# A graph layer on one core: five of 49 destination blocks gathered row by row, 44 packed

## The chip, the cores and the metric

The kernel runs on one core of a Trainium2 chip. The metric is the device time of one launch in microseconds (us). The other seven cores do nothing.

## The reference

One message-passing layer with two edge types, a residual and a layer norm, over N = 6250 nodes of 128 features and E = 100,000 edges sorted by destination:

```
Xs  = x[src]
msg = where(edge_type == 0, Xs @ W_data.T + b_data, Xs @ W_control.T + b_control)
agg = segment_sum(msg, dst)                      # per destination node
out = relu(agg + x @ W_self.T + b_self)
y   = layernorm(x + out)                         # per node, eps 1e-5
```

## The kernel before

**Blocks and tables.** The nodes are cut into NB = 49 blocks of P = 128. In a lead-in, TensorE computes both message vectors of every node, `x @ W + b`, and the kernel splits each fp32 result into three bf16 parts. They lie side by side as 384 columns (D3) in SBUF, tile `m3[:, s, :]`, with NT = 98 source tiles: 49 blocks for each of the two edge types. A copy goes to DRAM as `table`, one row of 768 bytes per (type, node). The parts of x themselves are stored to DRAM as `x3_t`. `load_x`, `split_x`, `multiply`, `take`, `leave`, `store_x` and `store` are the lead-in; its pools close at the step `built`.

**Windows.** Since edges are sorted by destination, the edges of a destination block lie in a window of WIN = 2304 edges (KT = 18 columns of 128), whose first edge the kernel finds itself (`starts`). SP loads a window per block (`win`).

**Packing.** Blocks are worked in groups, `GROUPS = (4,) + (5,) * 9`. For each group the kernel builds a packing: one-hot tiles of the source tile of each edge (`hot_st`, line L548), a running rank of each edge among those with the same source tile (matmuls with `tri` and `rest` into `acc`, read by VectorE into `slot`, L565), and from these, with the matmuls of L603, the packed lists: for each source tile 32 slots, each with a source row and a destination row. ScalarE copies them (L616, L636), and SP stores `packed` to DRAM. Edges of rank 32 or more are listed as spills; GpSimd fetches their messages from `table` with an indirect DMA of 32 rows (`msg_s`, L693).

**A packed block.** SP broadcasts the block's packed list to all partitions (`rows`, 784 KB, L718). VectorE turns it into one-hot matrices (L725, `select`) and makes the destination's one-hots in two chunks (`hot_d`, L739, `to_hots`). Then come NS = 25 tiles. In each, four matmuls gather four source tiles' messages out of `m3` into a PSUM tile `g_ps` (L752, `gather`; GB = 5 buffers), ScalarE evicts it as bf16 `gs` (L760, `evict`), and four matmuls, one for each 32 columns of the array (`by_columns`, L220), add it into the block's sum `agg` (`add_up`). The block's own product `x @ W_self` is added from `x_p`, which SP loads from `x3_t` (L781, `load_own`, `own_of`); a last product adds spills and bias. VectorE adds the three parts (L142), adds x and relu (L138) into the group's tile `h_p` and takes its statistics. After a group, `normalise` applies the norm on ScalarE (L179), and SP stores `h_p` (L186).

**The order.** Each engine runs its instructions in order. Nothing in the program text fixes that order: the functions are generators of steps, and the class `Order` simulates five engines ("T", "V", "A", "G", "S" for TensorE, VectorE, ScalarE, GpSimd and SP) with costs written in each step. It always issues the step that can start earliest and, among those that can start within `CLOSE` of it on that engine, the one with the earliest due time (function `due`, from BUILT = 85 and BLOCK per block). A step names the steps that it needs; a step with two engines in its costs goes to the one that is free first. So the whole instruction stream of the chip follows from these costs and due times, and a transfer or an engine that is slower than planned holds up whatever stands behind it. The semaphores between engines follow from the buffers.

**Buffers.** The pool `late`, opened at `built`, has one buffer of each tile unless `bufs` is given: `h_p` has one, `x_p` and `xs_p` four (XS), `hot_d` four, `gs` eight. `rows` has four (RB). Each of the eight PSUM banks is in use: three for `small`, `acc` and `agg`, five for `g_ps`.

Of the kernel before, what the change touches and what calls it, by code (L numbers as in the profile page):

```python
# [19 lines left out]
P = 128  # L20
# [12 lines left out]

GROUPS = (4,) + (5,) * 9
Q = max(GROUPS)
NPG = len(GROUPS)
STARTS = [sum(GROUPS[:i]) for i in range(NPG)]
R = 32
NS = (NT + 3) // 4
NC = 4 * NS  # L40
RB = 4
M = 8
SLOT = 128.0
PARTS = (4, 8, 8, 8, 8, 8, 5)
KC = 6
DC = 13
# [3 lines left out]
class Order:  # L50
# [9 lines left out]
    AFTER = 0.25  # L60
    CLOSE = 0.2

# [38 lines left out]
def kernel(  # L101
# [24 lines left out]


    nc = tc.nc
    dram = ctx.enter_context(tc.tile_pool(name="dram", bufs=1, space=DRAM))
    const = ctx.enter_context(tc.tile_pool(name="const", bufs=1))  # L130
    table = dram.tile([NT * P, D3], BF16, name="table")
    x3_t = dram.tile([NB, D, 3 * P], BF16, name="x3_t")
    packed = dram.tile([NB, NT * R], BF16, name="packed")
    total = const.tile([1, 1], I32, name="total")
# [69 lines left out]
def sums_over_windows(ctx, tc, x, xt, edges, w, bias, table, x3_t, packed, total,  # L204
# [3 lines left out]
    const = ctx.enter_context(tc.tile_pool(name="consts", bufs=1))  # L208
    work = ctx.enter_context(tc.tile_pool(name="work", bufs=2))
    row_pool = ctx.enter_context(tc.tile_pool(name="row_pool", bufs=RB))  # L210
    ps_a = ctx.enter_context(tc.tile_pool(name="ps_a", bufs=1, space=PSUM))
# [30 lines left out]
    counted = {}  # L242
    for n in sorted({DC, *GROUPS}):
        counted[n] = const.tile([P, P, n], BF16, name=f"count{n}")
        G.iota(counted[n], pattern=[[1, P], [0, n]], base=0, channel_multiplier=0,
               allow_small_or_imprecise_dtypes=True)
# [34 lines left out]
    def three_parts(parts, whole, left):  # L281
# [17 lines left out]
    spill_tiles = [(const.tile([P, Q * P], BF16, name=f"hot_s{i}"),  # L299
                    const.tile([P, D3], BF16, name=f"msg_s{i}")) for i in range(2)]  # L300
    slot_values = [const.tile([P, (Q + 1) // 2, NC], BF16, name=f"vs{i}") for i in range(2)]
    slot_b = {n: const.tile([P, R, n], BF16, name=f"slot{n}") for n in sorted({*GROUPS})}

    def constants():
# [23 lines left out]

        for hot, msg in spill_tiles:
            V.memset(hot, 0.0)  # L330
            V.memset(hot[R : R + 1, :], 1.0)
            V.memset(msg, 0.0)
            V.tensor_copy(msg[R : R + 1, :].rearrange("p (i c) -> p i c", i=3),
                          parts[0:1, :, 2 * D :])

    win = {}
    first = const.tile([1, NB], I32, name="first")
    counts = const.tile([P, NPG], F32, name="counts")
    m3 = const.tile([P, NT, D3], BF16, name="m3")
    m3v = m3.rearrange("p (t b) c -> p t b c", t=2)  # L340

    def starts():
# [12 lines left out]
        V.tensor_scalar_min(first, first_ps[:1, :NB], float(E - WIN))  # L355
        for b in range(NB):
            grp = [g for g in range(NPG) if STARTS[g] <= b][-1]
            yield step(("win", b), {"S": 0.84}, "first", *([("fields", grp - 2)] if grp > 1 else []),
                       lag=2.0)
            if b == STARTS[grp]:  # L360
                win[grp] = work.tile([P, Q, KT, 3], I32, name="win")
            at = nc.values_load(
                first[0:1, b : b + 1], engines=(SP,), min_val=0, max_val=E - WIN,
                skip_runtime_bounds_check_because="it counts edges and is held to E - WIN",
            )
            nc.sync.dma_start(
                win[grp][:, b - STARTS[grp], :, :],
                edges[ds(at, WIN), :].rearrange("(p k) c -> p k c", p=P),
            )
# [8 lines left out]
    LEAD, BUILT = 12.0, 85  # L378
    BLOCK = 13.5
    AHEAD = 12.0  # L380

    def due(kind, *i):
        if kind in ("p", "g") and i[0] in ("root", "rooted", "scale", "apply", "out"):
            n = i[1] + 1
            return BUILT + 10 + BLOCK * sum(GROUPS[:n])
        if kind in ("counted", "turned", "first"):
# [13 lines left out]
        if kind in ("win", "xs", "agg", "o", "whole", "sum"):  # L400
            b = i[0]
            begun = BUILT + BLOCK * b
            if kind == "win":
                return begun - 2 * BLOCK * GROUPS[1] - 20
            return begun + {"whole": BLOCK + 0.5, "sum": BLOCK + 3}.get(kind, 0.3 * BLOCK)
        if kind in ("rows", "sel", "d", "g", "e", "s"):
            of = {"rows": 1, "sel": 1, "d": 2}.get(kind, NS)
            lead = {"rows": -9, "sel": -3, "d": -1, "g": 0, "e": 1, "s": 2}[kind]
            return BUILT + BLOCK * (i[0] + (i[1] / of if len(i) > 1 else 0)) + lead
        n = GROUPS[i[0]]  # L410
        end = BUILT + BLOCK * STARTS[i[0]] - AHEAD
# [14 lines left out]
    def load_x():  # L426
        for g, n in enumerate(PARTS):
            yield step(("xt", g), {"A": 0.45}, *([("x3", g - 3)] if g > 2 else []), lag=4.0)
            xts[g] = build.tile([D, max(PARTS), P], F32, name="xt", bufs=3)[:, :n]
            A.dma_start(xts[g].rearrange("p b c -> p (b c)"),  # L430
                        xt[:, at_part[g] * P : (at_part[g] + n) * P])
# [21 lines left out]
    def multiply():  # L453
        for i, (g, b, n) in enumerate(two_blocks):
            free = [("yl", two_blocks[i - YB][1])] if i >= YB else ["biased"]
            yield step(("y", b), {"T": 1.08 * n}, ("x3", g), *free)
            ys[b] = y = ps_y.tile([P, 2, 2 * D], F32, name="y")
            for j in range(n):
                for i in range(3):
                    for k in range(3):  # L460
                        T.matmul(y[:, j, :], x3s[g][:, b + j - at_part[g], i, :],  # L461
                                 w3[:, k, : 2 * D], start=i == j == k == 0, stop=False,
                                 skip_group_check=True)
                T.matmul(y[:, j, :], ones_b, bias3, start=False, stop=True, skip_group_check=True)  # L464

# [242 lines left out]
    d_hots, g_tiles, gs_tiles, aggs, xss, x3b, hs_, mvs = {}, {}, {}, {}, {}, {}, {}, {}  # L708
    XS = 4
    DB, EB, GB = 4, 8, 5  # L710

# [9 lines left out]
    def select():  # L721

        for b in range(NB):
            yield step(("sel", b), {"V": 1.2}, ("rows", b))
            V.tensor_scalar(rows[b], rows[b], pid1, None, op0=ALU.is_equal)  # L725

    def to_hots():
        tiles = [(b, c) for b in range(NB) for c in range(-(-NS // DC))]
        for i, (b, c) in enumerate(tiles):
# [12 lines left out]

    tiles = [(b, g) for b in range(NB) for g in range(NS)]

# [10 lines left out]
    def evict():  # L755
        for i, (b, g) in enumerate(tiles):
            free = [("s", *tiles[i - EB])] if i >= EB else []
            e = yield step(("e", b, g), {"A": 0.37}, ("g", b, g), *free)
            gs_tiles[b, g] = gs = late.tile([P, D3], BF16, name="gs", bufs=EB)
# [15 lines left out]

    def load_own(name, blocks):
        for i, b in enumerate(blocks):
            free = [("sum", blocks[i - XS])] if i >= XS else []
            yield step(("xs", b), {"S": 0.9}, ("rows", b), "built", *free, lag=4.0)
            x3b[b] = late.tile([D, 3, P], BF16, name=f"x3_{name}", bufs=XS)  # L780
            nc.sync.dma_start(x3b[b].rearrange("p i c -> p (i c)"), x3_t[b])  # L781
            xss[b] = load_rows(b, late, f"xs_{name}", XS)

    def own_of(blocks, begun):

        for i, b in enumerate(blocks):
            yield step(("agg", b), {"S": 0.0}, *([("whole", blocks[i - 1])] if i else []))
            yield step(("o", b), {"T": 0.5}, ("xs", b), begun(b))
            for i in range(3):
                by_columns(aggs[b].rearrange("p (i c) -> p i c", i=3), x3b[b][:, i, :],  # L790
                           w3[:, :, 2 * D :], start=False, stop=False, skip_group_check=True)

    def finish_blocks():
        for b, (grp, q) in enumerate(blocks):
# [3 lines left out]
            if q == 0:  # L798
                hs_[grp] = late.tile([P, Q, D], F32, name="h_p")
                mvs[grp] = work.tile([P, Q, 2], F32, name="mv_p")  # L800
# [16 lines left out]


    late = ps_g = None

    def close_build():
        nonlocal late, ps_g
        yield step("built", {"S": 0.0}, "stores", ("yl", NB - 1), *[("x3_t", g) for g in range(len(PARTS))])
        early.close()
# [9 lines left out]
        take(1, "ym", "y1"), leave(1, "y2", "ym"), take(2, "yl", "y2"), constants(), store_x(), store(), close_build(),  # L834
        load_own("p", list(range(NB))), own_of(list(range(NB)), lambda b: ("s", b, 0)),
    ], due)


    total_ps = ps_a.tile([P, 512], F32, name="small")
    T.matmul(total_ps[:1, :NPG], ones[:, 0:1], counts, start=True, stop=True)  # L840
    total_f = work.tile([1, 1], F32, name="total_f")
    V.tensor_reduce(total_f, total_ps[:1, :NPG], axis=AX.X, op=ALU.add)
    V.tensor_copy(total, total_f)
# [121 lines left out]
```

## Time and profile before

| | before |
|---|---|
| device time, median of three runs | 721.98 us (721.96 to 722.43) |
| the profiled execution | 718.77 us, its span 717.1 us |
| TensorE busy, weight loads | 667.4 us (93%), 574.3 us (80%) |
| VectorE, ScalarE, GpSimd busy | 527.5 us (74%), 572.6 us (80%), 23.3 us (3%) |
| granted TensorE clock | 0.99 |
| DMA | 73.05 MB, 102 GB/s on average |

Device time contains the span from the first to the last instruction and a little around it. Busy time is the time in which an engine executes; matmuls are pipelined, so a TensorE that is always busy can still be waiting for its partner engines between tiles. In the group lines, "out<-in" names the tiles, "x1225" counts instructions, then come the busy time and the mean duration of one in ns, and after the second bar the idle time just before them and who ended it. In the timelines, the first two numbers are start and duration in us, and the bracket at the end is idle time before the instruction and the one that ended it.

### The profile page before, as it was taken

Reading aid. Unit: us, or ns where it says so; the run is one execution under the profiler, and the core shown is the slowest. Engines: PE = TensorE matmul, PEld = TensorE weight load, DVE = VectorE, ACT = ScalarE, POOL = GpSimd, SP = SyncE. Lnnn points to the kernel's source line nnn. Section 1 sums busy time; section 2 is a strip of 40 time slices with the busy share of each in tenths; the row PEclk is TensorE's granted clock in tenths of the full one; section 3 lists DMA queues with packets and bytes.
Section 4 is the critical chain, followed back from the end, with each engine's and each line's share of the span. In section 5 each row is a group of like instructions: output and inputs, shape, how many; then the busy total and the mean of one; then the engine's idle time right before and its main releaser. Section 6 shows DMA issues by size and latency. Waiting matters only on the chain.

```text
span 717.1 us, 33878 instructions
## 1 busy us (share of the span) xinstructions
PE 667.4 (93%) x14698; PEld 574.3 (80%) x14698; DVE 527.5 (74%) x1101; ACT 572.6 (80%) x1407; POOL 23.3 (3%) x21
## 2 busy tenths in 40 slices
PE   3799979999999999999989989999999999999993
PEld 2667747898898888889878888998988897887882
DVE  8565568788869958886985888699689778657321
ACT  3666546889789887888978888898889888798994
POOL 4000000000000000000000000000000000001000
PEclk9999989999999999999999999999999999999997
DMA  5566564053006105301710530160062026006200
GB/s 162 163 209 217 165 212 155 9 170 124 11 15 243 52 3 193 108 8 45 222 42 4 202 97 9 42 235 24 4 222 76 4 92 201 7 4 222 75 4 23
DMA packets 57564, 73.05 MB, mean 102 GB/s; under 512 B 12292, under 2 KB 50191, under 8 KB 57359
## 3 DMA queue, kind: packets, MB, share of 16 engines
q1 hardware_dynamic: 55806, 66.70, 28.6%
q10 hardware_dynamic: 1154, 3.41, 1.5%
q8 instruction: 116, 1.90, 1.1%
q0 software_dynamic: 448, 0.72, 0.3%
q14 instruction: 40, 0.33, 0.2%
HBM read 52.85 MB, written 17.96 MB: 99 GB/s over the span
## 4 chain that ended last, share of the span: by engine, by line
PE 57%; DVE 24%; DMA 10%; ACT 3%; issue 3%; SPq 1%; DVEq 0%; ACTq 0%
PE agg L220 21%; PE g_ps L752 17%; PE acc L220 7%; PE small L603 5%; DVE slot L565 4%; DMA x_p<-x_t 4%; DMA out<-h_p 4%; PE y L461 4%; DVE hot_d L739 4%; DVE hot_st L548 3%; DVE two L586 3%; ACT h_p L179 2%; DVE rows L725 1%; DVE hr L581 1%; PE y L480 1%
## 5 line engine op out<-in xcount | busy, mean ns | idle before, releaser
L760 ACT CAST gs<-g_ps 128x384 bf16<-128x384 f32 x1225 | 489.5, 514 | 67.9 <-PE g_ps L752 61.5
L220 PE MATMUL agg<-gs,hot_d 128*32 128x384 bf16 x4900 | 407.1, 332 | 2.8 <-ACT gs L760 1.9
L752 PE MATMUL g_ps<-m,rows 128*32 128x384 bf16 x4900 | 399.9, 328 | 3.1 <-DVE rows L725 2.8
L220 PEld LDWEIGHTS <-hot_d 128*32 128x32 bf16 x4900 | 232.5, 137 | 28.4 <-issue 5.9
L752 PEld LDWEIGHTS <-rows 128*32 128x32 bf16 x4900 | 217.0, 137 | 22.6 <-issue 5.6
L565 DVE TENSOR_REDUCE slot<-acc 128x5 bf16<-128x490 f32 (+1 forms) x180 | 117.5, 653 | 78.7 <-PE acc L220 76.1
L739 DVE TENSOR_TENSOR hot_d<-count,to 128x1664 bf16<-128x1664 bf16 x98 | 104.6, 1068 | 11.4 <-PE agg L220 9.1
L220 PE MATMUL acc<-hot_st,rest 128*32 128x490 bf16 (+1 forms) x680 | 72.8, 375 | 13.7 <-DVE slot L565 13.2
L220 PE MATMUL acc<-hot_st,tri 128*32 128x490 bf16 (+1 forms) x720 | 77.7, 370 | 1.3 <-DVE hot_st L548 1.3
L548 DVE TENSOR_TENSOR hot_st<-count,st_b 128x2940 bf16<-128x2940 bf16 (+1 forms) x30 | 58.8, 1964 | 16.0 <-PE small L603 8.1
L473 ACT CAST m<-y 128x512 bf16<-128x512 f32 (+1 forms) x75 | 40.5, 580 | 31.7 <-PE y L464 23.8
L603 PE MATMUL small<-hot_st,two 128*32 128x98 bf16 x1764 | 64.9, 291 | 0.0
L461 PE MATMUL y<-w,x 128*128 128x256 bf16 x441 | 57.8, 279 | 6.1 <-DVE w L283 3.2
L603 PEld LDWEIGHTS <-two 128*32 128x32 bf16 x1764 | 60.4, 118 | 0.9 <-issue 0.2
L220 PEld LDWEIGHTS <-rest 128*32 128x32 bf16 x680 | 30.5, 96 | 34.1 <-issue 30.3
L461 PEld LDWEIGHTS <-x 128*128 128x128 bf16 x441 | 43.7, 100 | 13.3 <-issue 3.2
L725 DVE TENSOR_SCALAR rows<-rows,pid 128x3136 bf16<-128x3136 bf16 x49 | 50.2, 1024 | 4.0 <-DMA rows<-packed 3.9
L142 DVE TENSOR_REDUCE whole<-agg 128x128 f32<-128x384 f32 x49 | 27.1, 553 | 34.6 <-PE agg L220 33.3
L220 PE MATMUL agg<-w,x_p 128*32 128x384 bf16 x588 | 36.4, 327 | 4.0 <-DMA x_p<-x_t 3.6
L693 POOL DMA_INDIRECT msg_s<-table,row_i x10 | 14.7, 1475 | 630.1 <-PE g_ps L752 484.6
L220 PEld LDWEIGHTS <-x_p 128*32 128x32 bf16 x588 | 20.7, 97 | 9.2 <-DMA x_p<-x_t 5.4
L220 PEld LDWEIGHTS <-tri 128*32 128x32 bf16 x720 | 24.5, 97 | 2.8 <-issue 2.1
(123 smaller groups left out, 369.5 us busy)
## 6 DMA issues: line engine op xcount, KB each, us to landing
rows<-packed SPq DMA_DIRECT2D x49, 784.0 KB, 6.7
table<-m SPq DMA_DIRECT2D x10, 768.0 KB, 4.2
x_p<-x_t SPq DMA_DIRECT2D x49, 96.0 KB, 7.1
x_t<-x SPq DMA_DIRECT2D x5, 768.0 KB, 7.7
xs_p<-in_x SPq DMA_DIRECT2D x49, 64.0 KB, 6.5
xt<-in_xt ACTq DMA_DIRECT2D x5, 512.0 KB, 4.4
out<-h_p SPq DMA_DIRECT2D x8, 320.0 KB, 3.9
win<-in_edges SPq DMA_DIRECT2D x49, 27.0 KB, 1.9
```

Of the source, the lines that this page charges most:

```text
L142: nc.vector.tensor_reduce(whole, agg.rearrange("p (i c) -> p c i", i=3), axis=AX.X, op=ALU.add)
L220: T.matmul(out[c : c + 32], lhsT[:, c : c + 32], rhs, **flags)
L461: T.matmul(y[:, j, :], x3s[g][:, b + j - at_part[g], i, :], w3[:, k, : 2 * D], start=i == j == k == 0, stop=False, skip_group_check=True)
L473: A.copy(part_of(b, n, i), ys[b][:, :n, :].rearrange("p b (t c) -> p t b c", t=2))
L548: V.tensor_tensor(hot, counted[n][:, None, 1 : NT + 1, :].to_broadcast([P, KC, NT, n]), fields[grp][2][:, c * KC : c * KC + KC, None, :].t ...
L565: V.tensor_reduce(slots[grp][:, k, :], by_q, axis=AX.X, op=ALU.max)
L586: V.tensor_tensor(two[:, :, i], hr, f[:, ks, None, :].to_broadcast(wide), op=ALU.mult)
L603: T.matmul(vt[c0 : c0 + R, q // 2, :], two[:, k, i, :, q], hot[:, k, :, q], start=c == k == 0 and q < 2, stop=c * KC + k == KT - 1, skip_g ...
L725: V.tensor_scalar(rows[b], rows[b], pid1, None, op0=ALU.is_equal)
L739: V.tensor_tensor(hot, counted[DC][:, :, :n], places[grp][:, q, None, c * DC : c * DC + n].to_broadcast([P, P, n]), op=ALU.is_equal)
L752: T.matmul(g_ps[t * R : (t + 1) * R, :D3], rows[b][:, :, s], m3[:, s, :], start=True, stop=True)
L760: (A.copy if e == "A" else V.tensor_copy)(gs, g_tiles.pop((b, g))[:, :D3])
```

## The change

Five destination blocks (44 to 48) are no longer packed. For each of them GpSimd fetches the messages of its 18 edge columns, 128 rows of `table` at a time, with an indirect DMA into `msg` (three buffers); VectorE makes one-hots of the destinations, six columns at a time (`hot_g`); and four matmuls per column add them into a sum of its own, `agg_g`. The own product and the bias (from `hot_b`, `msg_b`) are added as before. Their windows are loaded after those of the first two groups. In the plan a gather takes 5.8 us of GpSimd (PACE), so that the 90 gathers are spread over 522 us of it. The five blocks are normalised and stored together.

The packed groups become `(4,) + (5,) * 8`. `agg_g` takes a PSUM bank, and `g_ps` has four. `rows` has three buffers, `xt` two. `x_p` and `xs_p` are in a pool of their own, opened at the start, and wait for the part of `x3_t` that they read and for an older tile, not for `built` and `rows`. `h_p` has two buffers. The bias matmuls of a pair of blocks come after the products of both, and the first pairs need the step `bias`, no longer `biased`. In the last group an eviction may go to VectorE. CLOSE goes from 0.2 to 0.1 and BLOCK from 13.5 to 13.2. The diff, cut to what matters:

```diff
-GROUPS = (4,) + (5,) * 9
+GROUPS = (4,) + (5,) * 8
+NPB = sum(GROUPS)
+NG = NB - NPB
-RB = 4
+XS = 4
+RB = 3
+CH = 6
-    CLOSE = 0.2
+    CLOSE = 0.1
...
+    own_pool = ctx.enter_context(tc.tile_pool(name="own_pool", bufs=1))
...
-        for b in range(NB):
-            grp = [g for g in range(NPG) if STARTS[g] <= b][-1]
-            yield step(("win", b), {"S": 0.84}, "first", *([("fields", grp - 2)] if grp > 1 else []),
-                       lag=2.0)
+        for b in [*range(STARTS[2]), *range(NPB, NB), *range(STARTS[2], NPB)]:
+            grp = [g for g in range(NPG) if STARTS[g] <= b][-1] if b < NPB else NPG
+            free = [("fields", grp - 2)] if 1 < grp < NPG else []
+            yield step(("win", b), {"S": 0.84}, "first", *free, lag=2.0)
...
-    BLOCK = 13.5
+    BLOCK = 13.2
+    PACE = 5.8
...
+        if kind in ("gh", "gm", "msg"):
+            k = i[1] * CH if kind == "gh" else i[1]
+            return BUILT + PACE * (i[0] * KT + k) + {"msg": 0, "gh": 2, "gm": 5}[kind]
...
-            yield step(("xt", g), {"A": 0.45}, *([("x3", g - 3)] if g > 2 else []), lag=4.0)
-            xts[g] = build.tile([D, max(PARTS), P], F32, name="xt", bufs=3)[:, :n]
+            yield step(("xt", g), {"A": 0.45}, *([("x3", g - 2)] if g > 1 else []), lag=4.0)
+            xts[g] = build.tile([D, max(PARTS), P], F32, name="xt")[:, :n]
...
-            free = [("yl", two_blocks[i - YB][1])] if i >= YB else ["biased"]
+            free = [("yl", two_blocks[i - YB][1])] if i >= YB else ["bias"]
...
+            for j in range(n):
                 T.matmul(y[:, j, :], ones_b, bias3, start=False, stop=True, skip_group_check=True)
...
-    DB, EB, GB = 4, 8, 5
+    DB, EB, GB = 4, 8, 4
...
-            e = yield step(("e", b, g), {"A": 0.37}, ("g", b, g), *free)
+            costs = {"A": 0.37, "V": 0.53} if b >= STARTS[-1] else {"A": 0.37}
+            e = yield step(("e", b, g), costs, ("g", b, g), *free)
...
-            free = [("sum", blocks[i - XS])] if i >= XS else []
-            yield step(("xs", b), {"S": 0.9}, ("rows", b), "built", *free, lag=4.0)
-            x3b[b] = late.tile([D, 3, P], BF16, name=f"x3_{name}", bufs=XS)
+            part = [g for g in range(len(PARTS)) if at_part[g] <= b][-1]
+            free = [("sum", blocks[i - bufs])] if i >= bufs else []
+            yield step(("xs", b), {"S": 0.9}, ("x3_t", part), *free, lag=4.0)
+            x3b[b] = own_pool.tile([D, 3, P], BF16, name=f"x3_{name}", bufs=bufs)
...
-                hs_[grp] = late.tile([P, Q, D], F32, name="h_p")
+                hs_[grp] = late.tile([P, Q, D], F32, name="h_p", bufs=2)
...
+    def gather_rows():
+        for i, (j, k) in enumerate(gathered):
+            free = [("gm", *gathered[i - MB])] if i >= MB else [*stored, "built", "idx"]
+            yield step(("msg", j, k), {"G": PACE}, *free, lag=3.0 - PACE)
+            msgs[j, k] = late.tile([P, D3], BF16, name="msg", bufs=MB)
+            G.indirect_dma_start(
+                out=msgs[j, k], out_offset=None, in_=table[:, :],
+                in_offset=bass.IndirectOffsetOnAxis(ap=idx[:, j, k : k + 1], axis=0),
+            )
+
+    def gathered_hots():
...
+            yield step(("gh", j, c), {"V": 0.55}, ("msg", j, c * CH), *free)
+            g_hots[j, c] = hot = late.tile([P, P, CH], BF16, name="hot_g", bufs=XB)
+            V.tensor_tensor(hot, counted[CH],
+                            rel_g[:, j, None, c * CH : c * CH + CH].to_broadcast([P, P, CH]),
+                            op=ALU.is_equal)
+
+    def gathered_sums():
+        for j, k in gathered:
+            free = [("agg", NPB + j)] if k == 0 else [("o", NPB + j)] if k == KT - 1 else []
+            yield step(("gm", j, k), {"T": 0.165}, ("msg", j, k), ("gh", j, k // CH), *free)
+            if k == 0:
+                aggs[NPB + j] = ps_a.tile([P, D3], F32, name="agg_g")
+            by_columns(aggs[NPB + j], g_hots[j, k // CH][:, :, k % CH], msgs.pop((j, k)),
+                       start=k == 0, stop=k == KT - 1, skip_group_check=True)
...
-        load_own("p", list(range(NB))), own_of(list(range(NB)), lambda b: ("s", b, 0)),
+        finish_gathered(), gathered_sums(), gathered_hots(), gather_rows(), gathered_fields(),
...
+        load_own("p", list(range(NPB)), XS),
+        own_of(list(range(NPB)), lambda b: ("s", b, 0)),
+        load_own("g", list(range(NPB, NB)), 2),
+        own_of(list(range(NPB, NB)), lambda b: ("gm", b - NPB, 0)),
```

`gathered_fields` computes the table rows (`idx`) and the destinations (`rel_g`) of the five windows with six VectorE instructions; `finish_gathered` is the counterpart of `finish_blocks`.

## The prediction

> **What bounds the kernel now.** I read the stage table first, because the page's shares average over a lead-in, a long middle and an end that have different limits. In the stage table (duration, then busy us of TensorE, its weight loads, VectorE, ScalarE, GpSimd, then clock and DMA) the cuts lie at the stores of finished groups:
>
> ```profile
> 171.71:233.01 61.30, 60.40 (x1460) 53.67 (x1455) 50.11 (x106) 53.05 (x135) 1.70 (x1) 1.00 0.28 95
> ...
> 357.03:420.76 63.73, 59.98 (x1438) 53.65 (x1432) 50.79 (x107) 52.80 (x135) 1.70 (x1) 1.00 0.27 89
> ...
> 657.00:705.00 48.00, 46.44 (x1012) 38.49 (x1009) 15.87 (x33) 47.55 (x124) 0.00 (x0) 1.00 0.15 47
> ```
>
> Seven inner groups of five blocks run from 171.71 to 605.68, so one costs 62.0 us; TensorE is busy for 60 of them, VectorE 50, ScalarE 53. **TensorE bounds the middle.** The last five blocks (657 to 705) have no next group to build: there ScalarE is busy 47.55 of 48.0, so **the PSUM evictions bound the end**. GpSimd is nearly free everywhere.
>
> The groups of instructions say what the two do:
>
> ```profile
> L760 ACT CAST gs<-g_ps 128x384 bf16<-128x384 f32 x1225 | 489.5, 514 | 67.9 <-PE g_ps L752 61.5
> L220 PE MATMUL agg<-gs,hot_d 128*32 128x384 bf16 x4900 | 407.1, 332 | 2.8 <-ACT gs L760 1.9
> L752 PE MATMUL g_ps<-m,rows 128*32 128x384 bf16 x4900 | 399.9, 328 | 3.1 <-DVE rows L725 2.8
> ...
> L693 POOL DMA_INDIRECT msg_s<-table,row_i x10 | 14.7, 1475 | 630.1 <-PE g_ps L752 484.6
> ```
>
> Per packed block that is 25 tiles of four gathering and four adding matmuls and 25 evictions. The chain of waits gives the dense pitch: `x20` of them in 0.81 us, so 0.162 us for four.
>
> Next, what TensorE loses. The timeline at a group's end and the list of waits show it:
>
> ```profile
> 357.03 0.39 SPq L186 DMA_DIRECT2D out<-h_p  x1
> ...
> 362.04 0.29 DVE L138 SCALAR_TENSOR_TENSOR h_p<-whole,xs_p 128x128 f32<-128x128 f32 x1 [2.60 <-ACT gs L760]
> ...
> 366.79 0.39 PE L220 MATMUL acc<-hot_st,rest 128*32 128x490 bf16 x4 [2.68 <-DVE slot L565]
> ```
>
> The single h_p buffer is still being stored when the next group's first block wants it. VectorE stands 2.60 us (it is named after ScalarE; the store's 4.89 us in the chain end at that moment), its queue slips, and the rank chain leaves TensorE idle for 2.68 us.
>
> Last, the start of the main loop and the only existing table gathers:
>
> ```profile
> 114.89 0.67 PE L220 MATMUL agg<-w,x_p 128*32 128x384 bf16 x12 [1.60 <-DMA x_p<-x_t]
> ...
> 155.90 0.87 POOL L693 DMA_INDIRECT msg_s<-table,row_i  x1 [39.63 <-DVE dq L689]
> 218.01 1.70 POOL L693 DMA_INDIRECT msg_s<-table,row_i  x1 [61.23 <-PE g_ps L752]
> ...
> 651.58 2.77 POOL L693 DMA_INDIRECT msg_s<-table,row_i  x1 [61.27 <-PE g_ps L752]
> ```
>
> The view of line L693 ends with the landing times of its ten transfers:
>
> ```profile
> DMA to landing us min/median/max: 2.7/6.5/7.0
> ```
>
> A gather of 32 rows takes GpSimd 0.87, 1.70 or 2.77 us and lands in 2.7 us on idle DMA engines and about 7 us in a burst of `rows` broadcasts.
>
> **What the Trainium skill says.** "SBUF — State Buffer", Who interferes with whom: GpSimd and a VectorE instruction in a 2-port mode exclude each other, the second to issue waits. The trace agrees for one side: the 2.77 us record lies over a hot_d compare and then the `rows` compare of 652.58. That compare took 1.02 us against its mean of 1.024, so VectorE lost nothing. "DMA: Bandwidth & Descriptors", Anatomy of one DMA — SWDGE (gpsimd) path: 2.0 us plus bytes over 436e3. For 24 KB that gives 2.06 us, near the 2.7 seen on idle engines. The same page, Issuing engines are not separate DMA queues: all queues share the 16 engines; the 7.0 us landings inside bursts agree. "Perfetto Trace Analysis", Identifying the Most-Contended Engine, warns that matmul busy time is no measure of headroom. So I count instructions times pitch below.
>
> **The change, part by part.** All against the profiled execution: span 717.1 us, its own time 718.77, which stands 0.4% under the median of 721.98.
>
> 1. *One inner group of five packed blocks goes*, with its build: −62.0 us.
>
> 2. *Five blocks are gathered.* TensorE gets per block 18 sums of four matmuls (18 × 0.162 = 2.92), the own product (3 × 0.162 = 0.49) and the bias (0.16): 3.57 us, so 17.9 for five, spread over some eight groups at 2.2 each. By counting, a packed group needs 125 × 0.325 + 15 × 0.162 + 0.8 + 35 × 0.21 (ranks) + 6.1 (L603) + 1 = 58.3 us, so 3.7 of the 62.0 are bubbles and ScalarE-paced stretches, which extra matmuls partly fill. I take +16, ends +12 and +20. VectorE gets 15 compares of 128x768 (nearest row, L581 hr near that size, 0.66 us) and five times 1.31 us of finishing, 16.5 us. It loses five blocks at about 9.6 (2 × 1.07 hot_d, 1.02 rows, 1.31 finishing, and a fifth of a group's slots, hot_st, two and fields): nothing on the path. ScalarE loses 125 evictions.
>
> 3. *GpSimd issues 90 gathers* of 128 rows, 98 KB. No such gather is in the trace. Below, 0.87 us if rows are free. From the two sizes seen (32 rows 0.87, the 49 rows of `er` 1.13) 15 ns a row gives an estimate of 2.3 us; above, four times the common 1.70 is 6.8. I take 2.3. The plan spaces them at 5.8 and its three buffers let gather i start when sum i−3 is done, some 16 us before sum i: 2.3 + 7 us fits twice over in idle engines, once in a burst. Sums wait in TensorE's in-order queue with all packed matmuls behind them, so a late one costs directly. Gathers cannot start before the tables land (issued at 101.26) and end near 607 of the plan, before the packed blocks do. Spill gathers queue behind them; those have a block's time to land. I take +2, ends 0 and +10.
>
> 4. *h_p gets two buffers*: VectorE's 4.8 us on the store and the 4.1 us misnamed go, and with them part of the 13.2 us that TensorE waits for slots. What is late next is the rank chain itself. −5, ends 0 and −9.
>
> 5. *VectorE shares the last group's evictions.* ScalarE needs 25 × 0.395 = 9.87 us a block (24 in 9.48 us); TensorE 25 × 0.325 + 0.65 = 8.78. TensorE becomes the bound: −4.5, ends 0 (VectorE is never chosen, or its 0.55 us eviction, as L142 takes for the same columns, delays hot_d) and −5.
>
> 6. *x of the first blocks in the lead-in*: the 1.60 us stall and its echo in VectorE's 2.00 us go; the `rows` wait of 2.83 us at 105.8 stays. −2, ends 0 and −4. The bias matmuls come last in their pair: TensorE first waits for x parts there, not for the bias, so 0, ends −0.5 and +0.5.
>
> 7. *The lead-in gets more to issue.* On SP five more windows at 0.84 us ahead of the others, and 12 loads of x, each behind its x_t store (7.7 us to land), with the window loads queued behind; on VectorE the six index operations (1.5 us); xt has two buffers, its third load now behind the first split (it has 8 us until 20.29). Cover: TensorE is full from 40 to 100. If the first windows slip, the hot_st of 34.1 is late and TensorE's 1.31 us idle there grows: +2, ends 0 and +4.
>
> 8. *Four g_ps banks and three rows buffers.* Four banks per 0.165 + 0.5 us round trip still allow 0.17 us a tile, half of what is needed; three rows tiles are two blocks or 24 us ahead of a 7 us load. +2, ends −1 and +5.
>
> Sum: −62.0 + 16 + 2 − 5 − 4.5 − 2 + 2 + 2 = −51.5. Span 665.6, time 667.3, and times 721.98/718.77: **670 us**.
>
> **Rivals.** *Gathers late in bursts*: each of eight bursts of `rows` (10 us of 62, DMA 90% busy) delays one or two sums, with the whole TensorE queue behind them. For: the DMA engines are shared, and 128 small rows are four times a spill. Against: 16 us of cushion. At 4 us per burst +32: about 700 us.
>
> *VectorE bound*: if GpSimd locks it out for 1.70 us per gather, 10.7 gathers a group add 18 to VectorE's 50 and a group takes 68 instead of 62: +50, about 720. Against: the unslowed 1.02 us compare.
>
> *GpSimd too slow, the other side*: at 6.8 us a gather (four times 1.70; the 2.77 shows that waits add) the 90 outlast the plan's spacing, and TensorE's in-order queue halts at each sum. From about 5.7 us on, each costs 90 × the excess: before's time is reached at 6.3 us, and 6.8 gives 670 + 99 = 769. For: VectorE is busy 50 of 62 us with instructions that can hold descriptors up. Against: the 15 ns a row.
>
> *The change does not do what it says*: VectorE is not chosen, or early x loads still wait: 676, inside the range.
>
> **How the numbers follow.** As summed 0.78; bursts 0.11; VectorE bound 0.04; GpSimd slow 0.07. A difference under 0.2% (1.4 us) is about what cannot be told here. Faster: 0.78 + 0.11 + 0.01 of the third = 0.90; same 0.01; slower 0.09. All favourable ends together give some 652, all adverse ones some 703; they will not come together, so 656 to 690, which leaves the upper half of the bursts and the two slow cases out.
>
> **What would show it.** Nine stores instead of ten, inner groups near 64 us; `msg<-table` x90 with GpSimd near 2 to 3 us each and few waits of the gathered sums on DMA; no wait of h_p on its store; VectorE casts of gs with a last stage of about 8.9 us a block; no 1.60 us wait for x_p. The prediction is wrong if GpSimd's gathers take over 5.7 us, if sums wait on msg for over 10 us in all, or if an inner group exceeds 66 us.

## The result and the profile after

The kernel after takes **709.29 us** (median of four, 708.20 to 711.02) against 721.97: a ratio of 0.983 (95% interval 0.981 to 0.985). It is faster by 12.7 us, where 52 were forecast, and lies far above the range. The profiled execution took 708.20 us, its span 706.5.

The stage table of the kernel after, cut at stores of finished groups (first line) and at the last group (second line), in the columns used before:

```profile
181.62:247.75 66.13, 63.64 (x1493) 56.92 (x1496) 52.42 (x112) 53.05 (x133) 14.13 (x12) 1.00 0.33 102
...
653.50:692.00 38.50, 36.95 (x818) 33.97 (x817) 30.03 (x66) 28.37 (x67) 0.00 (x0) 0.96 0.11 34
```

The last group has turned as forecast: TensorE is the bound there, and ScalarE has room. But an inner group takes 66.1 us, seven of them 66.3 on average: above the 66 named as the sign of a wrong prediction. TensorE is busy for 63.6 of it, 3.2 more than in a group before, with only 33 more matmuls.

The groups of instructions (busy time, mean ns, then the engine's idle time and what ended it):

```profile
L780 ACT CAST gs<-g_ps 128x384 bf16<-128x384 f32 x1059 | 435.2, 503 | 114.4 <-PE g_ps L771 72.3 <-PE acc L228 14.3 <-PE agg L228 9.4
L771 PE MATMUL g_ps<-m,rows 128*32 128x384 bf16 x4400 | 379.1, 331 | 11.9 <-ACT gs L780 6.1 <-DVE ls L702 4.7
L866 POOL DMA_INDIRECT msg<-table,idx x90 | 104.1, 1156 | 362.7 <-PE g_ps L771 163.6 <-PE agg_g L228 160.2 <-PE acc L228 25.6
```

and, with different shapes kept apart, VectorE's share:

```profile
L780 DVE CAST gs<-g_ps 128x384 bf16<-128x384 f32 x41 | 22.4, 555 | 9.2 <-PE g_ps L771 8.6
```

ScalarE has 166 fewer evictions and yet idles 114.4 us before them instead of 67.9, waiting for TensorE, while TensorE waits more for ScalarE. A gather of 128 rows costs GpSimd 0.95 us in the median, less than half of the 2.3 assumed, and GpSimd is idle most of the time. From TensorE's list of waits, whole run (in all, how often, the longest):

```profile
...
PE agg L228 <- ACT gs L780: 6.3, 15, 1.1
PE g_ps L771 <- ACT gs L780: 6.1, 15, 0.7
PE g_ps L771 <- DVE ls L702: 4.7, 1, 4.7
PE acc L228 <- DVE slot L585: 4.1, 8, 1.1
```

Before, `slot` stood at 13.2, `gs` at 1.9 and x_p at 3.6 us. The waits for slots have shrunk and those for x_p have gone, as forecast; 12.4 us of waiting for `gs`, in 30 pieces of up to 1.1 us, have come. No wait for a gathered row is in the whole list.

### The profile page after: what moved, and what is told of

It is laid out like the page before. It is cut to its first block, busy times and chain, and to the rows that moved or that the text cites. A ratio compares the mean times of both kernels' runs of the same rounds, so it can differ in the third digit from the quotient of the medians.

```text
span 706.5 us, 31728 instructions
## 1 busy us (share of the span) xinstructions
PE 642.1 (91%) x13702; PEld 556.6 (79%) x13702; DVE 522.3 (74%) x1089; ACT 516.8 (73%) x1238; POOL 130.0 (18%) x111
## 4 chain that ended last, share of the span: by engine, by line
PE 74%; DVE 9%; DMA 4%; ACT 4%; issue 2%; SPq 2%; ACTq 0%; DVEq 0%
PE agg L228 27%; PE g_ps L771 23%; PE acc L228 8%; PE small L623 7%; PE y L480 4%; DMA rows<-packed 4%; ACT gs L780 3%; PE agg_g L228 2%; DVE slot L585 1%; DVE two L606 1%; PE y L500 1%; DVE rows L744 1%; DVE hot_d L758 1%; ACT h_p L186 1%; DVE hr L601 1%
## 5 line engine op out<-in xcount | busy, mean ns | idle before, releaser
L780 ACT CAST gs<-g_ps 128x384 bf16<-128x384 f32 x1059 | 435.2, 503 | 114.4 <-PE g_ps L771 72.3
L771 PE MATMUL g_ps<-m,rows 128*32 128x384 bf16 x4400 | 379.1, 331 | 11.9 <-ACT gs L780 6.1
L228 PE MATMUL agg<-gs,hot_d 128*32 128x384 bf16 x4400 | 372.5, 333 | 11.5 <-ACT gs L780 6.3
L228 PEld LDWEIGHTS <-hot_d 128*32 128x32 bf16 x4400 | 226.0, 137 | 33.3 <-issue 22.6
L866 POOL DMA_INDIRECT msg<-table,idx x90 | 104.1, 1156 | 362.7 <-PE g_ps L771 163.6
L585 DVE TENSOR_REDUCE slot<-acc 128x5 bf16<-128x490 f32 (+1 forms) x162 | 105.6, 652 | 82.2 <-PE acc L228 60.5
L758 DVE TENSOR_TENSOR hot_d<-count,to 128x1664 bf16<-128x1664 bf16 x88 | 93.6, 1067 | 3.8 <-ACT to L656 2.3
L228 PE MATMUL acc<-hot_st,tri 128*32 128x490 bf16 (+1 forms) x648 | 70.2, 370 | 0.0
L623 PEld LDWEIGHTS <-two 128*32 128x32 bf16 x1584 | 54.0, 118 | 5.8 <-DVE two L606 2.7
L149 DVE TENSOR_REDUCE whole<-agg 128x128 f32<-128x384 f32 x44 | 24.4, 554 | 23.3 <-PE agg L228 12.4
L713 POOL DMA_INDIRECT msg_s<-table,row_i x9 | 13.5, 1495 | 145.9 <-DVE slot L585 101.9
L228 PE MATMUL agg_g<-msg,hot_g 128*32 128x384 bf16 x360 | 37.4, 330 | 0.4 <-DVE hot_g L878 0.2
```

Source lines behind the costliest of these rows:

```text
L149: nc.vector.tensor_reduce(whole, agg.rearrange("p (i c) -> p c i", i=3), axis=AX.X, op=ALU.add)
L228: T.matmul(out[c : c + 32], lhsT[:, c : c + 32], rhs, **flags)
L585: V.tensor_reduce(slots[grp][:, k, :], by_q, axis=AX.X, op=ALU.max)
L623: T.matmul(vt[c0 : c0 + R, q // 2, :], two[:, k, i, :, q], hot[:, k, :, q], start=c == k == 0 and q < 2, stop=c * KC + k == KT - 1, skip_g ...
L758: V.tensor_tensor(hot, counted[DC][:, :, :n], places[grp][:, q, None, c * DC : c * DC + n].to_broadcast([P, P, n]), op=ALU.is_equal)
L771: T.matmul(g_ps[t * R : (t + 1) * R, :D3], rows[b][:, :, s], m3[:, s, :], start=True, stop=True)
```

## Where TensorE stops

One of those pieces, in the timeline of the kernel after (start, duration, then the idle time before it and what ended it):

```profile
316.73 0.95 POOL L866 DMA_INDIRECT msg<-table,idx  x1 [5.57 <-PE g_ps L771]
...
317.03 0.98 PE L771 MATMUL g_ps<-m,rows 128*32 128x384 bf16 x16
...
318.10 0.56 DVE L149 TENSOR_REDUCE whole<-agg 128x128 f32<-128x384 f32 x1 [0.77 <-PE g_ps L771]
318.21 0.86 ACT L780 CAST gs<-g_ps 128x384 bf16<-128x384 f32 x2 [0.64 <-PE g_ps L771]
...
318.74 0.39 PE L771 MATMUL g_ps<-m,rows 128*32 128x384 bf16 x4 [0.73 <-ACT gs L780]
```

TensorE runs four g tiles from 317.03, one about every 0.2 us. VectorE waits for a sum that ended at about 317.2, ScalarE for the first of these tiles. Both are released only at 318.1, 0.4 us after the end of the gather, and TensorE, out of free g_ps banks, then waits for ScalarE. The matmuls ran in time; their signals did not come. The trace's record of TensorE's semaphore shows it, with the same gather in a later run of **the same kernel** (e15 below) under it:

```
updates of TensorE's semaphore, us
after  gather 316.73 to 317.68: 316.48 316.64 316.96                      318.07 318.13 318.19 318.25 318.31
e15    gather 308.21 to 309.15: 307.95 308.12 308.44 308.76 308.93 309.09 309.25 309.51 309.94
```

In the first, five updates are held, the first by 0.9 us, and then appear 0.06 us apart, faster than the 0.16 us at which tiles follow each other densely. The timeline of e15 has no wait at this place:

```profile
307.69 2.94 ACT L780 CAST gs<-g_ps 128x384 bf16<-128x384 f32 x7
...
308.21 0.94 POOL L866 DMA_INDIRECT msg<-table,idx  x1 [5.58 <-PE g_ps L771]
...
308.47 2.15 PE L771 MATMUL g_ps<-m,rows 128*32 128x384 bf16 x25
...
308.79 0.56 DVE L149 TENSOR_REDUCE whole<-agg 128x128 f32<-128x384 f32 x1
```

I call this a **stop**. It lies at 65 of the 90 gathers of the kernel after (an update over 0.35 us late, against the modelled end of its matmul, that appears between 0.2 us after the gather's start and 0.6 us after its end); the latest is 1.1 us late. In the series without stops no update at a gather is more than 0.40 us late. Another measure needs no model of a matmul's end: between 0.4 and 1.25 us after the start of a gather (90, with nine of the spills and that of `er`), the kernel after shows 96 updates in all, e15 shows 242. The expectations below count `er` in and say 91.

Only TensorE's updates are seen to be late: of VectorE's and ScalarE's at the same gathers, each that is on record comes within 0.1 us of its instruction's end. Some 80 of theirs near the gathers are missing from the record of the kernel after, so this is not certain.

## Experiments

They ran in five series, each on one chip, the kernel before beside each; all medians in us. In a series either all kernels show stops or none does.

| series | updates per gathers, stops | kernels |
|---|---|---|
| the first | 96 per 100, stops | after 709.29 |
| e1 to e4 (before 718.83) | e3: 100 per 100, stops | 725.49, 710.85, 706.01, 694.18 |
| e5 to e8 (before 719.57) | e8: 243 per 100, none | 711.42, 706.17, 681.96, 687.65 |
| e9 to e12 (before 719.80) | e9: 98 per 100, stops | 709.99, 709.69, 713.84, 696.20 |
| e13 to e16 (before 720.13) | e15: 242 per 100, none | 695.35, 685.71, 686.17, 684.63 |
| e17, e18 (before 718.40) | e18: 224 per 100, none | 693.98, 677.82 |

### Single steps of the change, put into or taken out of a kernel

**e1**, four g_ps banks in the kernel before:

```diff
-    DB, EB, GB = 4, 8, 5
+    DB, EB, GB = 4, 8, 4
```

> The kernel before with four g_ps banks instead of five, nothing else. Theory A (the bank that agg_g took is what lengthens the inner groups: TensorE waits for ScalarE to free a g_ps bank): inner groups go from 62.0 to about 65 to 66 us, so 25 to 35 us over the whole, 747 to 757 us. Theory B (the gathered sums and fetches themselves disturb the groups; four banks are enough): 722 to 727 us.

725.49 us, ratio 1.010 (1.007 to 1.014): the banks cost 7 us alone, not the 30 of the theory that they are the main cause.

**e2**, two h_p buffers in the kernel before, and **e10**, the same again:

```diff
-                hs_[grp] = late.tile([P, Q, D], F32, name="h_p")
+                hs_[grp] = late.tile([P, Q, D], F32, name="h_p", bufs=2)
```

> The kernel before with two h_p buffers, nothing else. If the wait of VectorE on the store of h_p is on the path, as the prediction had it: its 8.9 us and the TensorE stalls behind it (1.6 to 2.5 us in each of eight groups) go, 705 to 714 us. Rival (the rank chain is late anyway): 719 to 722 us.

> The kernel before with two h_p buffers, unchanged, once more; the first time its ten spill gathers stopped TensorE's updates 9 times in 10. Theory (session): no stops now, and some 3 to 7 us less than the 710.85 of then, 703 to 708 us. Rival (the kernel decides): stops again at 9 of 10 spill gathers, 709 to 712 us.

710.85 us, 0.990 (0.986 to 0.994), and 709.69, 0.985 (0.981 to 0.990). TensorE's wait for slots falls from 13.2 to 2.5 us in e2. The step is worth 8 to 10 us. Both series had stops, at nine of the ten spill gathers, so e10 could not tell series from kernel.

**e6**, three rows buffers (`RB = 3`) in the kernel before, and **e5**, which adds to this the two h_p buffers, the four banks, CLOSE and BLOCK of the change, without gathering:

```diff
-RB = 4
+RB = 3
```

> The kernel before with three rows buffers instead of four, nothing else. The stalls of VectorE on rows in the kernel after (2 to 5 us at three of the places) come either from the third buffer's late release or from what was queued on SP. Theory (the buffer alone is worth little here: two blocks ahead of a 7 us load): +0 to +3 us, 720 to 723 us beside a before of 720. Rival (three buffers are the cause of the long first blocks of a group): +8 us or more, 728 us and up, with VectorE waits on rows at most group starts.

> The kernel before with everything of the change that is not gathering: two h_p buffers, four g_ps banks, three rows buffers, and the order's two constants (CLOSE 0.1, BLOCK 13.2). Theory (the missing 40 us come with the gathered steps in the order of issue; the tighter buffers alone cost little): the parts add up, -8 for h_p, +7 for the banks, 0 to +5 for rows and constants, so 717 to 725 us beside a before of 720, and TensorE's waits for ScalarE's gs stay under 12 us. Rival (the tighter buffers cost it wherever they are, and only their combination shows it): some 25 to 30 us above the 711 of two h_p buffers alone, so 735 to 745 us, with waits for gs near 20 us and half-clock stretches of 10 us.

e6 took 706.17 us, 0.982 (0.979 to 0.986): 13 us *less*, which no theory had. The later `rows` step changes the order of VectorE's instructions; no wait of h_p on its store of 0.5 us or more is left, though h_p has one buffer, and the wait for slots is 3.0 us. e5 took 711.42, 0.990 (0.986 to 0.993): 8 us saved, where e2, e1 and e6 add up to some 14. So the tighter buffers alone are not what went wrong, and effects of single edits do not add where an edit reorders a queue.

**e3**, the kernel after without the iota of the six-column count tile:

```diff
-    for n in sorted({DC, CH, *GROUPS}):
+    for n in sorted({DC, *GROUPS}):
...
-            V.tensor_tensor(hot, counted[CH],
+            V.tensor_tensor(hot, counted[DC][:, :, :CH],
```

> The kernel after without the added count tile of six: hot_g compares with the first six columns of the count tile of 13. Theory A (VectorE's begun stood 8.5 us against GpSimd's iotas, and all the lead-in behind it): the first matmul comes some 7 us earlier and the kernel ends about 7 us earlier, 701 to 703 us. Rival (the lead-in is bound by transfers or by the later chain and catches up): 707 to 710 us.

The timeline of the lead-in, first of the kernel after, then of e3:

```profile
1.76 10.29 POOL L253 IOTA count<- 128x512 bf16 x4
3.58 8.52 DVE L274 TENSOR_SCALAR begun<-bound_f,r0f 125x49 f32<-125x49 f32 x1
12.15 0.33 PE L276 MATMUL small<-ones,begun 125*49 125x1 f32 x2 [12.15 <-DVE begun L274]
```

```profile
1.76 6.38 POOL L253 IOTA count<- 128x512 bf16 x3
3.68 1.13 DVE L274 TENSOR_SCALAR begun<-bound_f,r0f 125x49 f32<-125x49 f32 x1
4.86 0.33 PE L276 MATMUL small<-ones,begun 125*49 125x1 f32 x2 [4.86 <-DVE begun L274]
```

With the fourth iota, the comparison `begun` lasts until the last iota ends; in e3 only until the second of them ends, at 4.76 (a VectorE instruction of its size took 0.17 us just before). Why it is let go in the one case and not in the other is not shown. In e3 TensorE starts 7.3 us earlier; the first g tile gains 3.8 of it (109.6 to 105.8, the time of the kernel before), and the whole 3: 706.01, with an interval (0.978 to 0.987) that overlaps that of the kernel after.

**e4**, the kernel after with 6 of the 18 columns of each gathered block fetched and summed, spaced at 17.4 us:

> The kernel after with 6 instead of 18 edge columns per gathered block (60 of the 90 fetches and sums left out, so the sums of these five blocks are incomplete), spread over the same time. Theory A (banks): only the matmul work of 60 sums goes, 60 x 0.162 = 9.7 us, and a little of the waits: 696 to 702 us. Theory B (the gathers disturb the groups): two thirds of the excess of 4.6 us per group go, some 25 us, 680 to 688 us.

694.18 us, 0.966 (0.962 to 0.969), beside e3 in one series. 60 gathers are worth some 12 to 15 us; 9.7 of that is their TensorE work. I took it for proof that gathers were cheap. It was not: its order differs (the first blocks of its groups take 18.2 us on average, from one `whole` to the next, 15.6 in the kernel after), its granted clock was half in six stretches of 27.2 us together (three of 13.6 us in the kernel after), and stops remain at nearly half of its 30 gathers.

**e8**, the kernel after with ScalarE alone in the last group, and **e11**, the same again:

```diff
-            costs = {"A": 0.37, "V": 0.53} if b >= STARTS[-1] else {"A": 0.37}
+            costs = {"A": 0.37}
```

> The kernel after with ScalarE alone evicting in the last group, as before the change. Theory (sharing works in the last group: blocks of 9.1 us instead of 9.8, but the first block of the group loses 3.9 us for another reason): +2 to +4 us, 711 to 713 us beside an after of 709, last blocks at 9.7 to 9.8 us. Rival (VectorE's share delays the compares and sums that start the last group, and is what costs the 3.9 us there): 0 to -3 us, the first block of the last group back near 12.5 us.

> The kernel after with ScalarE alone evicting in the last group, unchanged, once more, beside the kernel after in the same session. Theory (session): the two differ by what VectorE's share in the last group is worth, 0 to 4 us, whichever state the session is in. Rival (the kernel decides): 686 to 689 us and 20 us or more under the kernel after again.

e8 took 687.65 us, against the 709.29 of the kernel after, although up to the last group the two are the same instruction for instruction: the difference grew all through the groups before. e11 took 713.84. The groups of ScalarE's evictions, e8 and then e11:

```profile
L780 ACT CAST gs<-g_ps 128x384 bf16<-128x384 f32 x1100 | 444.3, 509 | 84.8 <-PE g_ps L771 48.1 <-PE acc L228 15.2 <-PE agg L228 7.8
```

```profile
L780 ACT CAST gs<-g_ps 128x384 bf16<-128x384 f32 x1100 | 448.1, 512 | 106.1 <-PE g_ps L771 67.2 <-PE acc L228 14.3 <-PE agg L228 7.8
```

One program, 26 us apart; in e8 no update at a gather is over 0.36 us late, in e11 some 63 of the 90 gathers have stops. Within a series VectorE's share is worth 3.9 us (e11 against e9) or, from two series without stops, 1.5 (e8 against e15).

### The stops, and what is left without them

**e9** and **e15**, the kernel after again:

> The kernel after, unchanged, once more. In its first profile TensorE's semaphore updates stop for about 0.7 us during 65 of the 91 gathers of 128 rows (none of the updates due in the gather's last half appears until 0.35 us after its end); in the kernel with ScalarE alone in the last group, whose instructions are the same up to that group, the updates go on through the gathers and the time was 687.65 us. Theory (the stop is not in the kernel's instructions but in something that differs from one loading or session to another, so the pair of sessions differs): now without stops, 683 to 689 us. Rival (the stop belongs to this kernel, for instance by where its data or its instructions lie): 706 to 712 us with stops at over 50 gathers.

> The kernel after, unchanged, as the measure for the three beside it. Theory (stops come and go with the series of runs, not with the kernel): 706 to 712 us with stops at 60 to 70 of 91 gathers, or, without stops, 681 to 688 us; the three others follow. Rival (it comes with one loading of a program): no relation to the other three runs.

709.99 us, 0.986 (0.982 to 0.990), with stops at some 65 of the 90 gathers; then 686.17, 0.952 (0.948 to 0.957), with no update at a gather over 0.36 us late. It goes with the series, not with the kernel. The group of the slot reads, of the kernel after and of e15, is the plainest sign in an ordinary view:

```profile
L585 DVE TENSOR_REDUCE slot<-acc 128x5 bf16<-128x490 f32 (+1 forms) x162 | 105.6, 652 | 82.2 <-PE acc L228 60.5 <-PE g_ps L771 20.8
```

```profile
L585 DVE TENSOR_REDUCE slot<-acc 128x5 bf16<-128x490 f32 (+1 forms) x162 | 105.5, 651 | 68.1 <-PE acc L228 63.7 <-PE g_ps L771 3.8
```

A slot read needs `acc`. That it is released by a g tile for 20.8 us fits an update that came in a bunch with later ones.

**e13** and **e17**, plain loads in place of the 90 gathers:

```diff
-            G.indirect_dma_start(
-                out=msgs[j, k], out_offset=None, in_=table[:, :],
-                in_offset=bass.IndirectOffsetOnAxis(ap=idx[:, j, k : k + 1], axis=0),
-            )
+            nc.sync.dma_start(msgs[j, k], table[i * P : (i + 1) * P, :])
```

> The kernel after with each of the 90 gathers replaced by a plain load of 128 neighbouring rows of the table, issued by SyncE at the same place of the order (the sums of the five gathered blocks then take the wrong rows; the instructions of TensorE, VectorE and ScalarE are the same). Theory (GpSimd's gathers stop TensorE's updates, and that is 26 us): if the kernel after, run beside it, shows stops, this one is 20 to 28 us under it, 682 to 690 us, without stops but at the spill gathers; if it shows none, the two are within 3 us. Rival (gathers are only where the stops show; the cause is something else): within 5 us of the kernel after in either case, with stops at other times.

> The kernel after with the 90 gathers replaced by plain loads of SyncE (the gathered blocks take the wrong rows), unchanged, once more; it took 695.35 us beside a kernel after without stops (686.17). Theory (only GpSimd's gathers can stop TensorE's updates): 693 to 698 us again, whatever the kernel beside it shows; if that one shows stops, only the nine spill gathers add some 2 to 4 us here. Rival (the stops come without gathers too): 710 to 720 us where the kernel beside it shows stops. If that one shows none, the run tells nothing new.

695.35 and 693.98 us, both in series without stops, so the question that they were made for, whether the stops vanish with the gathers inside a series that has them, stays open. Beside a kernel after without stops the loads cost 9 us *more*, and GpSimd's gathers are the better way here. TensorE's sums now wait for rows, which they do in none of the other runs (e13, then e17):

```profile
PE agg_g L228 <- DMA msg<-table: 14.4, 9, 4.2
```

```profile
PE agg_g L228 <- DMA msg<-table: 12.1, 7, 4.3
```

Why the loads come late is not shown; they stand in SP's queue with all other loads.

**e14**, every gather issued twice, the second into a tile that nothing reads:

```diff
+            spare = late.tile([P, D3], BF16, name="spare", bufs=2)
+            G.indirect_dma_start(
+                out=spare, out_offset=None, in_=table[:, :],
+                in_offset=bass.IndirectOffsetOnAxis(ap=idx[:, j, k : k + 1], axis=0),
+            )
```

> The kernel after with every gather of 128 rows issued twice, the second into a spare tile that nothing reads (180 gathers, the rest as it was). Theory: if the kernel after, run beside it, shows stops, +15 to +30 us over it, with stops at most of the added gathers too; if it shows none, +0 to +3 us. Rival (the stops come from the landing or the summing of the rows, not from GpSimd's work): +0 to +5 us with stops at the same number of places.

685.71 us against 686.17 (e15): without stops, 90 more gathers of 128 rows cost nothing that can be measured.

### The order

**e7** and **e16**, evictions planned at 0.44 us:

```diff
-            costs = {"A": 0.37, "V": 0.53} if b >= STARTS[-1] else {"A": 0.37}
+            costs = {"A": 0.44, "V": 0.53} if b >= STARTS[-1] else {"A": 0.44}
```

> The kernel after with one number of the order changed: an eviction on ScalarE is planned at 0.44 us instead of 0.37 (on the chip it takes 0.39 to 0.41 with its issue). The instructions and buffers are the same, only their order differs. Theory (the order is too optimistic on evictions, so TensorE meets unfinished gs tiles after each gathered sum): TensorE's waits for gs fall from 20.5 us to under 10 and the time to 695 to 702 us. Rival (these waits come from the buffers, not from the order): within 3 us of the kernel after, 706 to 712 us, with gs waits near 20 us.

> The kernel after with evictions planned at 0.44 us, beside the kernel after. It had 681.96 us in the series without stops. Theory (the order's cost of an eviction is a cause of its own, and helps more where TensorE's updates come late): with stops 697 to 702 us, 8 to 13 us under the kernel after; without stops 680 to 684 us, 1 to 4 us under it. Rival (its gain was that series' alone): within 2 us of the kernel after.

e7's 681.96 us, 27 under the kernel after, looked like the answer; its gain was nearly all that of a series without stops. Beside e15, e16 took 684.63: 1.5 us less, inside the intervals (0.945 to 0.953 and 0.948 to 0.957).

**e12** and **e18**, this cost and e3's edit together, the fastest version found:

> The kernel after with two changes: evictions planned at 0.44 us, and no iota of its own for the gathered compare, which reads the 13-column count tile instead (the iotas held VectorE's first comparison for 8.52 us). If stops are absent: 681.96 of the eviction cost alone less 1 to 4 us for the lead-in, 678 to 681 us, first g tile near 105.5 us instead of 109. If stops are present: 690 to 705 us. Rival on the lead-in (the main phase gives it back, as it did where only the iota was taken out): no gain over 682.

> The kernel after with evictions planned at 0.44 us and without an iota of its own for the gathered compare, unchanged, once more; with stops it took 696.20 us where the kernel after took 709.99. Theory: with stops 695 to 698 us; without stops 678 to 682 us, 1 to 4 us less for the lead-in than the eviction cost alone (681.96 and 684.63). Rival (the order's cost only helps against stops, and the lead-in is given back): without stops 684 to 688 us, as the kernel after.

With stops 696.20 us, 0.966 (0.962 to 0.971), 13.8 under e9; e3's edit accounts for about 3 of it, so the order is worth some 10 where updates come late. Without stops 677.82, 0.943 (0.938 to 0.948): 6.8 under e16, 3.8 of it in the lead-in (first g tile at 105.6 instead of 109.4).

## Why the prediction was wrong

The budget, from the profiled spans (before 717.1, after 706.5, e15 683.6). TensorE's time is cut at each matmul's start; of a step to the next one, what exceeds 0.25 us is counted as waiting, the rest as a step of the matmul that begins it.

| us against before | predicted | e15, no stops | after |
|---|---|---|---|
| lead-in, to the first g tile | +2 | +4.5 | +3.8 |
| packed blocks, without waits (step 1) | -62 | -59.1 | -50.0 |
| gathered sums, own products, bias (step 2) | +16 | +18.8 | +18.4 |
| TensorE's waits (the net of steps 3, 4, 5, 6, 8) | -7.5 | -1.8 | +13.0 |
| from the last sum to the end | 0 | +4.2 | +4.2 |
| sum | -51.5 | -33.4 | -10.6 |

That e15's 686.17 us lies inside the stated range, 656 to 690, is luck: two thirds of the forecast gain came, and most terms are off.

**The step that failed is 3.** It bounded the gathers by GpSimd's own time and by landing and gave them +2, at most +10. Both bounds held (0.95 us instead of 2.3; no sum stood for a row), but a third cost was not thought of: while GpSimd works on a gather, TensorE's semaphore updates can be held. Between e15 and the kernel after, the same program, lie 22.9 us of span: 14.7 as waits and 9 as slightly longer steps (of these at most some 3 are the granted clock, which was half for 13.6 us from about the start of the main loop on, and for 10.2 in e15). The spill gathers could not have warned: in the profile before, which has no stops, its eleven gathers show 15 updates, but only 2 and 3 where e2 and e1 ran. A cost that depends on the series cannot be bounded from one trace.

**Step 3 missed the end too** (+4.2): GpSimd's closing instructions, an INC_SWDGE_SEM and a DRAIN, take 0.40 and 0.97 us before, 2.19 and 8.23 after 90 gathers, 0.98 and 3.33 in e4, 0.38 and 0.88 in e13. They end last, 9.6 us after the last store is issued.

**Step 1** was mis-sized by 3 even without stops: the 62.0 of a group include waits that stay when a group goes; its own count of 58.3 was the nearer figure to subtract. **Step 2** was too small by 3: its count of 17.9 was nearer to the 18.8 than the 16 that it took for bubbles partly filled. **Step 4** was right in kind and too small: h_p is gone from the waits, 8 to 10 us instead of 5. But the waits in sum fell by 1.8 only, since others came: in e15's list 4.7 us of sums that wait for VectorE's `whole`, and 1.6 more for `gs`. In each of the four cases VectorE had stood for `rows` 1.5 to 4.5 us earlier; these waits have grown (before, then e15):

```profile
DVE rows L725 <- DMA rows<-packed: 3.9, 4, 2.8
```

```profile
DVE rows L744 <- DMA rows<-packed: 16.2, 10, 4.6
...
PE agg L228 <- DVE whole L149: 4.7, 4, 2.1
```

**Step 5** held in its mechanism: the last four blocks take 9.1 to 10.6 us, against 9.9 to 11.3 with ScalarE alone (e8, e11), and the share is worth 1.5 to 3.9 us instead of 4.5. The first of that group takes 16.3 instead of 12.4, but it does so without VectorE's share too (16.0 in e8, 17.3 in e11). **Step 6** held: x_p is in no list of waits, though `rows` now stands 4.6 us at that place instead of 2.8. **Step 7** had the right sign and the wrong cause: not SP's queue but the fourth iota; without it (e3) the first g tile comes as early as before. The Trainium skill's "SBUF — State Buffer", Who interferes with whom, says that the lock is held for a whole instruction and the other side fully blocks; the prediction had quoted it for the gathers. At the iotas the trace agrees that VectorE is blocked, but not for one instruction only: 8.52 us, across three iotas. **Step 8**: the banks cost 7 us in the kernel before, the rows buffers there -13; but that three rows tiles are far enough ahead did not hold in e15, as the 16.2 us above show. The third buffer alone is not the reason: in e6 these waits are 4.3 us.

Of the rivals, late gathers, a locked VectorE (its `rows` compare took 1.03 us, as before) and a slow GpSimd all fell, and the change does what it says. (The adverse ends of the eight steps together give 699 us, not 703; nothing rests on it.)

**Open.** What makes a series one with stops; two on the same chip were of different kinds. That the gathers cause the stops rests on their place, 0.4 us after a gather's end in kernels with 30, 90 or 10 of them, and not on a run that takes them away while a series has them. A matmul's end is modelled in the trace, so it stays open too whether the update itself is held or the results that it reports. And why `rows` comes late with the gathered blocks was not looked into.

## What to carry to other kernels

Before costing an instruction on a nearly idle engine at its own duration, ask what it holds up on the others: compare when a producer's matmul ended with when its consumers were released. If two kernels with the same instructions up to a point already differ before it, run the same kernel again in another series before believing any edit. And subtract from a stage its counted work, not its length.

## What the runs showed of the hardware

- TensorE's semaphore updates can be held during a GpSimd gather and come 0.06 us apart from 0.4 us after its end on. With 90 gathers, series with these stops are 23 to 26 us longer than series without.
- A gather of 128 rows of 768 bytes takes GpSimd 0.95 us in the median (up to 2.9), one of 32 rows 0.87 to 2.77; the rows are no measure.
- GpSimd's closing DRAIN took 8.23 us after 90 gathers and 6.60 after 180 (e14), but 0.97 with ten of 32 rows.
- A VectorE comparison lasted 8.52 us across three of GpSimd's iotas, and 1.13 us beside the end of one; an instruction of its size took 0.17 us.
